# Attention and gated low-rank layer on one core: key operands prepared a chunk ahead, and several side tasks placed at other points

## The chip, the cores and the metric

The kernel runs on one core of one Trainium2 chip. The metric is the device time of one execution in microseconds, as the median of several executions. A profile was taken of one execution; its times start at the first instruction.

## The reference

The input x is (2, 2048, 2048) in float32, that is 4096 tokens of width 2048. All weights are float32.

```python
xn = layernorm(x)                                   # no gain, no bias
# attention, one head of width 512, over 2048 keys of the same batch
q, k, v = split(xn @ Wqkv + bqkv)                   # each (2, 2048, 512)
a = softmax(q @ k^T / sqrt(512)) @ v
attn = a @ Wo + bo
# feed-forward: 64 experts of rank 8, 16 chosen for each token
s = (xn @ Wq^T) @ keys^T                            # (.., 64)
gate = softmax over the 16 greatest of s, 0 elsewhere
z = (xn @ A^T) * repeat(gate, 8)                    # (.., 512)
ffn = (z @ B^T) * 2
out = x + attn + ffn
```

## The kernel before

**Numbers.** Every matrix product is made of float32 operands split into a high part (ScalarE's cast, `split_hi`, line 121 of the profile) and a low part (VectorE's subtraction, `split_lo`, line 124), and of three passes on TensorE (hi by lo, lo by hi, hi by hi). So each operand costs one ScalarE and one VectorE instruction before TensorE can use it.

**Blocks and fast products.** The tokens are 8 blocks of 512. Blocks 0 and 1 go through plain products. The other six go in three pairs (`PAIRS`), each by a scheme that needs seven block products in place of eight (`PHASES`, in the order P1, P2, P6, P5, P3, P7, P4). A phase is six tiles of q, k and z and one of values (`"V"`); beside the products, `beside(j, ph)` gives a list of steps for VectorE and ScalarE, dealt out after each of the phase's seven items.

**Scores.** After the projections, the scores of a pair of query blocks against a pair of key blocks use the same scheme. Their operands are prepared ahead and stored in DRAM. `key_steps(kb, d)` makes those of one chunk, half d of key block kb: two loads (`kr<-k_d`), then for each of seven steps a cast and a subtraction into a tile `kst`, four VectorE sums between them, and seven stores (`kp_d<-kst`), each issued at the next step. There are 16 chunks. `query_steps(j, ring)` makes the query sums of pair j (four loads, four sums, four stores for each half d, tile `qs`). `query_load` and `query_split` bring the operands of one query step into `qt`, and `key_load` brings `kt`.

**The main loop.** The loop over g runs one score product each time (six matmuls of 512 columns, line 1062), 56 for each query pair (NG1 = 56), four pairs. From g = 65 on, `weigh` runs the products of the softmax weights with the values of the pair before (line 129, `acc<-ph,vt`) between them, two or three for one score; value tiles `vt` are loaded three ahead (`load_v`), the weights `ph` are made two ahead (`soft`). The dictionary `side` holds steps to be run after score g; `deal(g, steps, every)` puts them there. `maxes(blk)` finds each query's greatest score on VectorE, and `spread(blk)` is a TensorE product that spreads it over the partitions (tile `mq`, line 1115); `soft` needs the result. After the last score only `weigh` is left (the last values), and beside it `moving` loads and splits the weights of the output stage (`wo`, `wb`) and `ahead` its inputs (`xz`, `s`). `combos` makes sums of output weights for it.

**Queues and order.** Each engine runs its instructions in the order of the program, and nearly all loads and stores are issued by SyncE (SP) in one queue. The order is made by a recording layer from the order of the calls and its own estimates. `behind("sp")`, `behind("pe")` keep what is recorded inside from going ahead of the last instruction so named.

**Slots.** The SBUF memory is a fixed set of named slots (B, 1024 words; G; h and H, about 512). A `Ring` hands them out in turn; a tile that takes a slot waits until the last user of the tile before is done, so a slot that a store still reads holds up its next writer. The ring of the loaded keys is `ks["R"]` (two slots), that of `kst` is `ks["st"]`, that of the values leaving the last phases is `r_vs`. TensorE writes to seven PSUM banks (`acc`).

Of the kernel before, what the change touches and what calls it, by code (L numbers as in the profile page):

```python
# [62 lines left out]
def attn_ffn_kernel(ctx: ExitStack, tc, x, xT, wq, wv, wob, bqk, bv, bo, keysT, out):  # L63
# [17 lines left out]
    def big(*js):  # L81
        return Ring(sb, *(f"B{j}" for j in js))
# [577 lines left out]
    def beside(j, ph):  # L660

        b00, b01, b10, b11 = (0, 0), (0, 1), (1, 0), (1, 1)
        more = j + 1 in PAIRS
        s0, s1 = stat_steps.get(2 * j + 2), stat_steps.get(2 * j + 3)
        if ph == "P1":
            t3 = sum_steps(j, nc.vector, b01, b11, b01, ALU.subtract)
            n10, n01, n11 = x_steps(j, *b10), x_steps(j, *b01), x_steps(j, *b11)
            if j > PAIRS[0]:
                return [], mixed(split_steps(j, "P2", *b10), n01[1], n11[1], t3)
            return (  # L670
                [n10[0], n01[0], n11[0]],
                mixed(n10[1], split_steps(j, "P2", *b10)) + mixed(n01[1], n11[1]),
            )
        if ph == "P2":
            t3 = sum_steps(j, nc.vector, b01, b11, b01, ALU.subtract) if j == PAIRS[0] else []
            return [], mixed(
                t3, sum_steps(j, nc.vector, b00, b01, b00, ALU.add), split_steps(j, "P6", *b00)
            )
        if ph == "P6":
            return [], mixed(  # L680
                sum_steps(j, nc.vector, b10, b10, b00, ALU.subtract),
                sum_steps(j, nc.vector, b00, b11, b00, ALU.subtract), split_steps(j, "P5", *b00),
                s0[:-2] if more else key_steps(0, 0) + key_steps(0, 1) + key_steps(1, 0),
            )
        if ph == "P5":
            if more:
                steps = mixed(split_steps(j, "P3", *b11), s1[:-2])
                return [], s0[-2:-1] + steps[:6] + s0[-1:] + steps[6:]
            return [], mixed(
                split_steps(j, "P3", *b11),  # L690
                [st for m in range(3, 8) for st in key_steps(m // 2, m % 2)],
            )
        if ph == "P3":
            if more:
                n = x_steps(j + 1, *b00)
                steps = mixed(split_steps(j, "P7", *b01), n[1][:2])
                return n[0], s1[-2:-1] + steps[:3] + s1[-1:] + steps[3:]
            return [], mixed(split_steps(j, "P7", *b01), query_steps(0, big(*GROUPS[3])))
        if ph == "P7":
            if more:  # L700
                n = x_steps(j + 1, *b10)
                return n[0], mixed(split_steps(j, "P4", *b10), n[1][:2])
            return [], mixed(split_steps(j, "P4", *b10), query_steps(1, big(*GROUPS[2])))
        if more:
            return x_steps(j + 1, *b01)[0] + x_steps(j + 1, *b11)[0], mixed(
                x_steps(j + 1, *b00)[1][2:], split_steps(j + 1, "P1", *b00)[:2],
            ) + mixed(split_steps(j + 1, "P1", *b00)[2:], x_steps(j + 1, *b10)[1][2:])
        ks["st"] = big(18, 19)
        return [], [lambda: query_load(0, 0)] + mixed(
            [lambda n=n: query_ready(0, n) for n in range(7)], key_steps(4, 0) + key_steps(4, 1)  # L710
        )

    XU, YU, XV, YV = {}, {}, {}, {}
# [106 lines left out]
    ORDER = ("P1", "P6", "P2", "P5", "P3", "P7", "P4")  # L820
    NPAIR = NB // 2
    NKS = NK // 2
    ks = {"R": big(25, 26), "st": big(27, 28, 29, 9)}
    qop, kop = {}, {}

    def key_steps(kb, d):


        v = {}

        def load():
            for h in range(2):
                v[h] = ks["R"]([P, T], F32, "kr")
                nc.sync.dma_start(v[h], k_d[kb][h][:, d, :])
# [27 lines left out]
        return [load] + [lambda step=step: one(step) for step in steps] + [out]  # L862

    def query_steps(j, ring):
# [23 lines left out]
        return steps(0) + steps(1)  # L888

    def query_load(j, n):  # L890

# [97 lines left out]
    for j in PAIRS:  # L989
        for ph in PHASES:  # L990
            if j == PAIRS[-1] and ph == "P4":
                sA, sB, sC, sD = GROUPS
                r_qt = big(*sC, *sD, *sA, *sB)
                r_kt = big(*T_SLOTS[:3], 25, 26)
            n = phase(j, ph, n)


# [11 lines left out]
    r_tp = mid(0, 1, 2, 3)  # L1009
    r_ph = wide(0, 1, 2)  # L1010
    r_vt = wide(3, 4, 5, 9)
    ks = {"R": mid(0, 1), "st": wide(0, 1, 2, 3, 4, 5)}
    S, tag_of, mbc, pt_, M, L, av, rl_, vt_, lsum = {}, {}, {}, {}, {}, {}, {}, {}, {}, {}
    ones = mid(2)([P, P], F32, "ones")
    nc.vector.memset(ones, 1.0)
# [384 lines left out]
        for k, st in enumerate(steps):  # L1400
            side.setdefault(g + k * every, []).append(st)

    for n, (kb, d) in enumerate(((5, 0), (5, 1), (6, 0), (6, 1))):
        deal(2 + 11 * n, key_steps(kb, d))

    def small_ring():
        ks["st"] = mid(2, 3)

    deal(NG1 + 10, [small_ring] + key_steps(7, 0) + key_steps(7, 1))
    deal(NG1 + 38, query_steps(2, r_tp), 2)  # L1410
    deal(2 * NG1 + 7, query_steps(3, r_tp), 2)
    slots = [NG1 + 51, *(2 * NG1 + k for k in (20, 37, 43, 49)), *(3 * NG1 + k for k in (7, 13, 19))]
    for k, g in enumerate(slots):
        deal(g, combos(k // ND, k % ND), 2)

    for j in range(1, NPAIR):
        deal(NG1 * j - 14, [lambda j=j: query_load(j, 0), lambda j=j: query_split(j, 0)], 4)
        for n in range(1, 7):
            deal(NG1 * j - 7 + n, [lambda j=j, n=n: query_load(j, n), lambda j=j, n=n: query_split(j, n)], 3)
    deal(begin[0] - 8, [lambda c=c: load_v(c) for c in range(3)])  # L1420
    deal(begin[0] - 3, [lambda c=c: soft(c) for c in range(2)])
    done = 0
    for g in range(begin[-1]):
# [6 lines left out]
            with behind("sp"):  # L1430
                st()
        if j and j <= NPAIR:
            if n == 1:
                maxes(2 * j - 2)
            if n in (0, 2):
                with behind("pe"):
                    spread(2 * j - 1 - n // 2)
        if n == NG1 - 2 and j < NPAIR:
            maxes(2 * j + 1)
        for i in range(NPAIR - 1):  # L1440
# [20 lines left out]
    slots = [*qt_, *b_[2:], *ph_, *vt2_[:3]]  # L1461
    r_tm = [slots_of(*slots[4 * n : 4 * n + 4]) for n in range(len(STEPS))]
    r_xo = half(0, 1, 2, 3, 4, 5, 6, 7)
    while done < NW * NPAIR:
        weigh(done)
        done += 1
        c, d = divmod(done - NW * (NPAIR - 1), ND)
        if d == 0 and c in (2, 6, 10, 14):
            for kk in range(0, ND, 2):
                with behind("sp"):  # L1470
                    for st in moving(0, STEPS[c // 4], kk):
                        st()
        if d == 0 and c == 18:
            load_bo(0)
        if d == 0 and c in (20, 24, 28):
            ahead(c // 4 - 5)
# [75 lines left out]
```

## Time and profile before

| | |
|---|---|
| median of 3 runs | 2652.06 us (2650.37 to 2656.02) |
| profiled execution | 2654.26 us, span 2652.4 us from first to last instruction |
| mean granted TensorE clock | 0.991 |
| TensorE busy with matmuls | 2604.3 us, 98% |
| VectorE, ScalarE, GpSimd busy | 1982.9, 858.9 and 519.9 us |
| projections, last pair from phase P6 on | 1110 to 1333 us of the span |
| scores alone (g = 0 to 64) | 1333 to 1450 us |
| scores and weighting by turns | 1450 to 1924 us |
| last values | 1924 to 2039 us |
| output stage | 2039 us to the end |

How to read the rows that follow later. A row of the timeline has its start in us, its length, the engine, the line of the kernel, the operation, output<-inputs, and the number of instructions merged; in square brackets is how long the engine sat idle before it and what ended that. A row of the waits has who waited, for whom, the total in us, how often, and the longest. A row of a table by stretches has the busy time (and number of instructions) of TensorE, its weight loads, VectorE, ScalarE and GpSimd, then the granted clock, the share of the DMA engines and GB/s.

### The profile page before, as it was taken

The numbers are of one execution on the slowest core, as the hardware profiler recorded it, in microseconds if no ns is written. First come the engines' busy times: TensorE is split into PE (matmuls) and PEld (weight loads), VectorE is DVE, ScalarE is ACT, GpSimd is POOL, SyncE is SP. The second block draws the span as 40 slices with busy tenths as digits, with TensorE's granted clock in tenths as the row PEclk, the third lists the DMA queues.
The fourth block names the chain that finished last, engine by engine and source line by source line (L and its number), as shares of the span: only waits on it lengthen the run. The fifth ranks groups of instructions, "written<-read, shape, count | busy, mean of one in ns | idle before, by whom it ended". The sixth has DMA issues, their size and how long they took to land. (4 is left out here: it accounts for less than half of the span.)

```text
span 2652.4 us, 34800 instructions
## 1 busy us (share of the span) xinstructions
PE 2604.3 (98%) x12689; PEld 2197.6 (83%) x12689; DVE 1982.9 (75%) x2827; ACT 858.9 (32%) x1249; POOL 519.9 (20%) x315
## 2 busy tenths in 40 slices
PE   8999999999999999999989999999999999999999
PEld 7889888888888889888867887878877888888887
DVE  6557539867868678776778979979698766797675
ACT  4223223323332323343323423334254222232221
POOL 1311420001000010000000000000000756566654
PEclk9999999999999999999999999999999999999999
DMA  6667874667446673688999898888578545565542
GB/s 233 228 246 260 286 273 170 221 217 266 146 155 221 219 256 121 195 260 284 313 284 313 251 316 294 272 311 297 178 270 291 177 166 171 175 218 175 179 160 102
DMA packets 348043, 608.10 MB, mean 229 GB/s; under 512 B 28456, under 2 KB 151392, under 8 KB 347872
## 3 DMA queue, kind: packets, MB, share of 16 engines
q1 hardware_dynamic: 334912, 575.99, 65.0%
q10 hardware_dynamic: 12960, 29.89, 3.4%
q8 instruction: 100, 1.64, 0.3%
q14 instruction: 71, 0.58, 0.1%
HBM read 450.42 MB, written 155.35 MB: 228 GB/s over the span
## 5 line engine op out<-in xcount | busy, mean ns | idle before, releaser
L129 PE MATMUL acc<-t,pw 128*128 128x512 f32 x3024 | 696.1, 391 | 5.4 <-ACT t L121 4.6
L129 PEld LDWEIGHTS acc<-t,pw 128*128 128x128 f32 x3024 | 566.9, 188 | 124.1 <-ACT t L121 5.0
L1336 PE MATMUL acc<-wb,s 128*128 128x512 f32 x2688 | 609.4, 389 | 0.0
L1336 PEld LDWEIGHTS acc<-wb,s 128*128 128x128 f32 x2688 | 504.7, 188 | 104.6
L1320 POOL TENSOR_TENSOR xo<-xo,bo_bc 128x512 f32<-128x512 f32 x128 | 210.8, 1654 | 914.5 <-DMA bo_bc<-in_bo 609.6
L129 PE MATMUL acc<-ph,vt 128*128 128x512 f32 x1536 | 381.0, 393 | 6.1 <-DMA vt<-v_d 2.8
L1062 PE MATMUL acc<-qt,kt 128*128 128x512 f32 x1344 | 342.1, 397 | 16.9 <-ACT sp L1069 10.3
L129 PEld LDWEIGHTS acc<-ph,vt 128*128 128x128 f32 x1536 | 290.3, 190 | 69.7 <-ACT ph L121 3.1
L1062 PEld LDWEIGHTS acc<-qt,kt 128*128 128x128 f32 x1344 | 256.1, 192 | 77.0 <-ACT sp L1069 11.8
L121 ACT CAST pw<-pw 128x1024 fp32r<-128x1024 f32 (+1 forms) x168 | 177.7, 1058 | 343.7 <-PE acc L129 231.9
L124 DVE TENSOR_TENSOR pw<-pw 128x1024 fp32r<-128x1024 f32 (+1 forms) x168 | 214.2, 1276 | 71.9 <-ACT pw L121 68.8
L129 PE MATMUL acc<-xh,wh 128*128 128x512 f32 x1152 | 263.6, 390 | 0.0
L129 PEld LDWEIGHTS acc<-xh,wh 128*128 128x128 f32 x1152 | 215.6, 188 | 44.9
L129 PEld LDWEIGHTS acc<-pw,t 128*128 128x128 f32 x2016 | 247.3, 189 | 3.9 <-DVE yv L755 2.6
L129 PE MATMUL acc<-pw,t 128*128 128x264 f32 x2016 | 248.3, 285 | 2.3 <-DVE yv L755 2.3
L121 ACT CAST s<-xz 128x1024 fp32r<-128x1024 f32 x112 | 118.0, 1054 | 373.4 <-PE acc L1336 313.2
L124 DVE TENSOR_TENSOR s<-xz,s 128x1024 fp32r<-128x1024 f32 x112 | 170.1, 1520 | 43.5 <-ACT s L121 43.5
L124 DVE TENSOR_TENSOR wh<-wu,wh 128x512 fp32r<-128x512 f32 x96 | 81.0, 860 | 99.4 <-ACT wh L121 99.4
L518 POOL TENSOR_TENSOR zt<-zt,g 128x512 f32<-128x512 f32 x24 | 39.0, 1633 | 517.2 <-DMA g<-gd 285.1
L121 ACT CAST ph<-sp 128x512 fp32r<-128x512 f32 x128 | 78.9, 619 | 167.2 <-PE acc L129 161.1
L1325 DVE TENSOR_TENSOR xo<-xo,acc 128x512 f32<-128x512 f32 x128 | 86.9, 680 | 54.8 <-PE acc L1336 26.0
L121 ACT CAST t<-xq 128x1024 fp32r<-128x1024 f32 x84 | 88.0, 1051 | 94.3 <-DVE xq L648 41.0
(165 smaller groups left out, 2525.3 us busy)
## 6 DMA issues: line engine op xcount, KB each, us to landing
vt<-v_d SPq DMA_DIRECT2D x128, 512.0 KB, 4.7
kt<-kp_d SPq DMA_DIRECT2D x224, 256.0 KB, 5.4
pw<-sq_d SPq DMA_DIRECT2D x72, 512.0 KB, 4.1
xo<-in_x SPq DMA_DIRECT2D x128, 256.0 KB, 3.2
xz<-oz_d SPq DMA_DIRECT2D x64, 512.0 KB, 4.5
out_y<-xo SPq DMA_DIRECT2D x128, 256.0 KB, 2.5
kp_d<-kst SPq DMA_DIRECT2D x112, 256.0 KB, 3.7
pw<-in_wq SPq DMA_DIRECT2D x54, 512.0 KB, 4.3
```

The costliest lines, as they stand in the source:

```text
L121: return nc.scalar.copy(hi, src)
L124: return (eng or nc.vector).tensor_tensor(lo, src, raw(hi), ALU.subtract)
L129: last["pe"] = nc.tensor.matmul(ps, st(a_), mv(b_), start=first and n == 0, stop=end and n == 2)
L518: nc.gpsimd.tensor_tensor(zt, zt, gx[n], ALU.mult)
L1062: last["pe"] = nc.tensor.matmul(ps, k[:, a, d, :], q[c][:, d, :], start=not more and d == 0 and i == 0, stop=d == 1 and i == 2, skip_group ...
L1320: nc.gpsimd.tensor_tensor(xs, xs, bo_bc[q // (NB // 2 * NH), c], ALU.add)
L1325: nc.vector.tensor_tensor(xs, xs, ps, op)
L1336: nc.tensor.matmul(ps, st[a_][:, kk, sl], mv[b_], start=not more and kk == 0 and n == 0, stop=kk == ND - 1 and n == 2, skip_group_check=more,)
```

## The change

- `key_steps` gives its load apart from its steps. The ring of loaded keys gets four slots (B25, B26, H7, H8 in the projections; the four h slots in the first 56 scores; two again from g = NG1 + 2). `key_list` puts the load of the next chunk after the third step of the chunk before. In the main loop a chunk's load stands three scores ahead of its first step (six for chunks 9 to 11).
- The chunks are spread differently: phases P6, P5, P3, P7, P4 of the last pair had 3, 5, 0, 0 and 2 of them and now have 3, 2, 0, 2 and 1 (`kst` gets three slots in P4 instead of two). The main loop takes 8 instead of 6: four in the first 56 scores as before, then chunks 12, 13 and 14 in the next 56, and 15 at the start of the third 56.
- The query sums of pair 0 are split over P3 and P7 (they were all in P3), those of pair 1 move from P7 to P4 and its end, in the four h slots.
- In P4 the values leave through `r_ev`, four slots, instead of two.
- `maxes` of the even block comes one score later (n = 2, not 1); `spread` comes at n = 1 and 4, not 0 and 2.
- The splits of pair 1's query operands come five scores after their loads, not three (the first five, not four).
- `combos` and the later `query_steps` run their three steps at distances 3 and 1 instead of 2 and 2, at other scores: five of the eight `combos` now fall after g = 168, where three did.
- The eight output loads of `moving` before the output stage come singly, at c = 1, 3, .. 15 of the last values, and their splits three values later, at c = 4, 6, .. 18; before, two loads with their splits came together at c = 2, 6, 10 and 14.

```diff
 def beside(j, ph):   # the last pair's branches
-                s0[:-2] if more else key_steps(0, 0) + key_steps(0, 1) + key_steps(1, 0),    # P6
+                s0[:-2] if more else key_list(0, 3),
-                [st for m in range(3, 8) for st in key_steps(m // 2, m % 2)],                # P5
+                key_list(3, 5)
-            return [], mixed(split_steps(j, "P7", *b01), query_steps(0, big(*GROUPS[3])))    # P3
+                split_steps(j, "P7", *b01), query_steps(0, big(*GROUPS[3]), (0,))
-            return [], mixed(split_steps(j, "P4", *b10), query_steps(1, big(*GROUPS[2])))    # P7
+                split_steps(j, "P4", *b10), query_steps(0, big(*GROUPS[3]), (1,)), key_list(5, 7)
-        ks["st"] = big(18, 19)                                                               # P4
+        ks["st"] = Ring(sb, "H6", "B18", "B19")
-            [lambda n=n: query_ready(0, n) for n in range(7)], key_steps(4, 0) + key_steps(4, 1)
+            [lambda n=n: query_ready(0, n) for n in range(7)],
+            key_list(7, 8, False) + query_steps(1, mid(0, 1, 2, 3)),
...
-    ks = {"R": big(25, 26), "st": big(27, 28, 29, 9)}
+    ks = {"R": Ring(sb, "B25", "B26", "H7", "H8"), "st": big(27, 28, 29, 9)}
+    def key_list(a, b, more=True):
+        for k in range(a, b + 1):
+            if k not in KEYS:
+                KEYS[k] = key_steps(k // 2, k % 2)
+        steps = [KEYS[a][0]] if a == 0 else []
+        for k in range(a, b):
+            ops = list(KEYS[k][1])
+            if k + 1 < b or more:
+                ops.insert(3, KEYS[k + 1][0])
+            steps += ops
+        return steps
...
+                r_vs = r_ev                       # from P4 of the last pair on
...
-    ks = {"R": mid(0, 1), "st": wide(0, 1, 2, 3, 4, 5)}      # main loop
+    ks = {"R": mid(0, 1, 2, 3), "st": wide(0, 1, 2, 3, 4, 5)}
...
-    for n, (kb, d) in enumerate(((5, 0), (5, 1), (6, 0), (6, 1))):
-        deal(2 + 11 * n, key_steps(kb, d))
+    def keys(k, g, load):
+        first, steps = key_steps(k // 2, k % 2)
+        deal(load, [first])
+        deal(g, steps)
+    def spaced(g, steps):
+        for k, st in enumerate(steps):
+            deal(g + (0, 3, 4)[k % 3] + 5 * (k // 3), [st])
+    for n in range(4):
+        keys(8 + n, 3 + 11 * n, 11 * n - 3 if n else 0)
-    deal(NG1 + 10, [small_ring] + key_steps(7, 0) + key_steps(7, 1))
-    deal(NG1 + 38, query_steps(2, r_tp), 2)
-    deal(2 * NG1 + 7, query_steps(3, r_tp), 2)
-    slots = [NG1 + 51, *(2 * NG1 + k for k in (20, 37, 43, 49)), *(3 * NG1 + k for k in (7, 13, 19))]
+    deal(NG1 + 2, [small_ring])
+    for n, g in ((12, NG1 + 6), (13, NG1 + 18), (14, NG1 + 49), (15, 2 * NG1 + 10)):
+        keys(n, g, g - 3)
+    spaced(NG1 + 36, query_steps(2, r_tp))
+    spaced(2 * NG1 + 19, query_steps(3, r_tp))
+    slots = [2 * NG1 + k for k in (35, 40, 45)] + [3 * NG1 + k for k in (7, 12, 17, 22, 35)]
     for k, g in enumerate(slots):
-        deal(g, combos(k // ND, k % ND), 2)
+        spaced(g, combos(k // ND, k % ND))
-        deal(NG1 * j - 14, [load of operand 0, split of operand 0], 4)     # lambdas, shortened
+        deal(NG1 * j - 14, [load of operand 0, split of operand 0], 5)
         for n in range(1, 7):
-            deal(NG1 * j - 7 + n, [load of operand n, split of operand n], 3)
+            deal(NG1 * j - 7 + n, [load of operand n, split of operand n], 5 if j == 1 else 3)
...
-            if n == 1:
+            if n == 2:
                 maxes(2 * j - 2)
-            if n in (0, 2):
+            if n in (1, 4):
                 with behind("pe"):
-                    spread(2 * j - 1 - n // 2)
+                    spread(2 * j - 1 - n // 4)
...
-        if d == 0 and c in (2, 6, 10, 14):
-            for kk in range(0, ND, 2):
-                with behind("sp"):
-                    for st in moving(0, STEPS[c // 4], kk):
-                        st()
+        if d == 0 and 1 <= c <= 18:
+            k, part = (c - 1) // 2, (c - 1) % 2
+            if part == 0:
+                if k < 8:
+                    half_of[k] = moving(0, STEPS[k // 2], 2 * (k % 2))
+                    with behind("sp"):
+                        half_of[k][0]()
+            elif k:
+                half_of[k - 1][1]()
```

More of the change, by code (lines that the diff above doesn't have):

```diff
@@ L688, in beside @@
                 return [], s0[-2:-1] + steps[:6] + s0[-1:] + steps[6:]
-            return [], mixed(
-                split_steps(j, "P3", *b11),
-                [st for m in range(3, 8) for st in key_steps(m // 2, m % 2)],
-            )
+            return [], mixed(split_steps(j, "P3", *b11), key_list(3, 5))
         if ph == "P3":
@@ L697, in beside @@
                 return n[0], s1[-2:-1] + steps[:3] + s1[-1:] + steps[3:]
-            return [], mixed(split_steps(j, "P7", *b01), query_steps(0, big(*GROUPS[3])))
+            return [], mixed(
+                split_steps(j, "P7", *b01), query_steps(0, big(*GROUPS[3]), (0,))
+            )
         if ph == "P7":
@@ L702, in beside @@
                 return n[0], mixed(split_steps(j, "P4", *b10), n[1][:2])
-            return [], mixed(split_steps(j, "P4", *b10), query_steps(1, big(*GROUPS[2])))
+            return [], mixed(
+                split_steps(j, "P4", *b10), query_steps(0, big(*GROUPS[3]), (1,)), key_list(5, 7)
+            )
         if more:
@@ L861, in key_steps, with query_steps @@
         steps = ("P1", "P2", "P4", "P5", "P7", "P6", "P3")
-        return [load] + [lambda step=step: one(step) for step in steps] + [out]
-    def query_steps(j, ring):
+        return load, [lambda step=step: one(step) for step in steps] + [out]
+    KEYS = {}
+    def key_list(a, b, more=True):
[9 more added lines that the diff above has]
+        return steps
+    def query_steps(j, ring, ds=(0, 1)):
         def steps(d):
@@ L886, in steps @@
             return [load, sums, out]
-        return steps(0) + steps(1)
+        return [st for d in ds for st in steps(d)]
     def query_load(j, n):
@@ L1401, in deal @@
             side.setdefault(g + k * every, []).append(st)
-    for n, (kb, d) in enumerate(((5, 0), (5, 1), (6, 0), (6, 1))):
-        deal(2 + 11 * n, key_steps(kb, d))
-    def small_ring():
-        ks["st"] = mid(2, 3)
-    deal(NG1 + 10, [small_ring] + key_steps(7, 0) + key_steps(7, 1))
-    deal(NG1 + 38, query_steps(2, r_tp), 2)
-    deal(2 * NG1 + 7, query_steps(3, r_tp), 2)
-    slots = [NG1 + 51, *(2 * NG1 + k for k in (20, 37, 43, 49)), *(3 * NG1 + k for k in (7, 13, 19))]
+    def keys(k, g, load):
[7 more added lines that the diff above has]
+        keys(8 + n, 3 + 11 * n, 11 * n - 3 if n else 0)
+    def small_ring():
+        ks["R"], ks["st"] = mid(0, 1), mid(2, 3)
+    deal(NG1 + 2, [small_ring])
[4 more added lines that the diff above has]
+    slots = [2 * NG1 + k for k in (35, 40, 45)] + [3 * NG1 + k for k in (7, 12, 17, 22, 35)]
     for k, g in enumerate(slots):
-        deal(g, combos(k // ND, k % ND), 2)
+        spaced(g, combos(k // ND, k % ND))
     for j in range(1, NPAIR):
-        deal(NG1 * j - 14, [lambda j=j: query_load(j, 0), lambda j=j: query_split(j, 0)], 4)
+        deal(NG1 * j - 14, [lambda j=j: query_load(j, 0), lambda j=j: query_split(j, 0)], 5)
         for n in range(1, 7):
-            deal(NG1 * j - 7 + n, [lambda j=j, n=n: query_load(j, n), lambda j=j, n=n: query_split(j, n)], 3)
+            deal(
+                NG1 * j - 7 + n, [lambda j=j, n=n: query_load(j, n), lambda j=j, n=n: query_split(j, n)],
+                5 if j == 1 else 3,
+            )
     deal(begin[0] - 8, [lambda c=c: load_v(c) for c in range(3)])
@@ L1463, in attn_ffn_kernel @@
     r_xo = half(0, 1, 2, 3, 4, 5, 6, 7)
+    half_of = {}
     while done < NW * NPAIR:
```

## The prediction

> **What bounds the kernel now.** First the page's busy rows: TensorE is busy 98%, and only it. Then TensorE's own waits, since only they can be won back:
>
> ```profile
> PE 2604.3 (98%) x12689; PEld 2197.6 (83%) x12689; DVE 1982.9 (75%) x2827; ACT 858.9 (32%) x1249; POOL 519.9 (20%) x315
> ...
> PE acc L1062 <- ACT sp L1069: 10.3, 3, 5.9
> PE misc L1115 <- DVE mq L1105: 4.7, 4, 1.8
> PE acc L129 <- ACT t L121: 4.6, 1, 4.6
> PE acc L1062 <- DVE qt L124: 4.4, 5, 1.3
> PE acc L129 <- DMA vt<-v_d: 2.8, 1, 2.8
> PE acc L129 <- DVE yv L755: 2.3, 1, 2.3
> ```
>
> Almost all of these lie between 1110 and 2039 us, where the change works. The timeline of the longest shows the mechanism:
>
> ```profile
> 1338.22 11.70 PE L1062 MATMUL acc<-qt,kt 128*128 128x512 f32 x42 [2.47 <-ACT sp L1069]
> ...
> 1346.42 0.43 DVE L288 TENSOR_TENSOR vs<-acc,xv 128x264 f32<-128x264 f32 x1 [7.53 <-DMA v_d<-vs]
> ...
> 1351.46 1.12 SPq L834 DMA_DIRECT2D kr<-k_d  x2
> ...
> 1354.90 0.40 ACT L121 CAST kst<-kr 128x256 fp32r<-128x256 f32 x1 [6.75 <-DMA kr<-k_d]
> 1355.21 0.58 ACT L1069 COPY sp<-acc 128x512 f32<-128x512 f32 x1
> ```
>
> VectorE waits 7.53 us because the third `vs` tile needs a slot that a store still reads (two slots). The key load is issued at 1351.46, when those same slots are free, and ScalarE waits 6.75 us for it at a `kst` cast. Behind the cast stands the copy of a score (L1069), which P2 of the next group must have: TensorE idles 5.92 us. Then the tables by stretches, for the cover:
>
> ```profile
> 1336.00:1346.00 10.00, 7.78 (x27) 6.34 (x28) 2.57 (x6) 1.33 (x4) 0.00 (x0) 0.83 0.97 299
> 1333.00:1390.00 57.00, 46.68 (x187) 36.33 (x186) 37.41 (x76) 13.27 (x32) 0.00 (x0) 0.91 0.90 284
> 1390.00:1450.00 60.00, 53.59 (x213) 41.12 (x212) 50.94 (x93) 19.78 (x33) 0.00 (x0) 0.95 0.94 323
> 1780.00:1850.00 70.00, 70.00 (x308) 57.72 (x309) 67.95 (x99) 26.93 (x37) 0.00 (x0) 1.00 0.88 300
> ```
>
> The granted clock falls after a gap; and VectorE, 37.4 + 50.9 = 88.3 us busy in the 117 us of scores alone, is nearly as loaded as TensorE: undisturbed, six matmuls start every 1.36 us, and 65 scores need 65 x 1.36 = 88.4 us.
>
> **What the skill says.** The Trainium skill, "TensorE: Matmul & The Clock Gate", Part 1, says that the clock halves after idling and that the windows are about 3.4 us. The trace agrees: a mean of 0.83 over 10 us is 1.7 us lost, 3.4 us at half. So I price a gap of about 2 us or more at itself **plus 1.7 us**. "PSUM — Partial Sum Buffer", Engine vs sequencer instructions, says that ScalarE and VectorE work in strict order; the L1069 row, free only after the `kst` cast, agrees. "DMA: Bandwidth & Descriptors", Issuing engines are not separate DMA queues, says that all transfers share the same 16 engines; before the 2.76 us gap at 1956 two `wo` loads of 512 KB stand among the `vt` loads, and the DMA engines are full (1.00 busy, 391 GB/s from 1956 to 1964), which fits.
>
> **The account of lost time**, from TensorE's timeline. The excess is the length of the run after a gap less (matmuls x 0.2267 us + 0.16), the pace of undisturbed runs.
> - P6 and P5: gaps 4.59 + 2.25, excess 2.3 + 0.8 = 9.9 us.
> - Scores alone: gaps 2.47 + 5.92 + 1.92 (ScalarE late), 1.85 (`kt`), 4.35 in five pieces (`qt` splits), excess 2.0 + 2.05 + 1.7 + 1.7 = 24.0 us.
> - By turns: `mq` 1.82 with 1.8 excess, 1.77 and 0.32, 0.26 after the first; 1.38 at 1530 behind a 3.35 us reciprocal. 7.35 us.
> - Last values: `mq` 0.76; `vt` 2.76 + 1.7; `ph` 1.92 + 1.8. 8.9 us.
>
> Together 50 us, the most that the change can win.
>
> **The change part by part.**
> *Key loads ahead, four slots, fewer chunks in P5.* No work is removed: 16 chunks of 7 casts and 11 VectorE operations of 0.42 us stay. The 51.3 us of ScalarE's wait for `kr` (21 times) should go, as a load (5.1 us to land) gets about five steps of a chunk, or three to six scores, of lead. In P5 the chunks fall from five to two, 3 x 4.6 = 13.8 us less on VectorE; P7, where VectorE was busy 29.8 of 45 us, takes 2 x 4.6 - 2.7 (query sums net) = 6.5 us more: covered. Won: 8 of 9.9.
>
> *Four value slots and early key loads at the start of the scores.* The third `vs` no longer waits, the key loads no longer need the `vs` slots, and in the changed program's order no `kst` cast stands between the value casts and the first score copy. Of 2.47 + 5.92 + 2.0 + 2.05 = 12.4 I take 10. The 1.92 + 1.7 was the same wait at the third chunk (7.38 us for `kr`): 3.5. The `kt` gap, 1.85 + 1.7, began with SP held from 1402 to 1406 by a `kst` store waiting for a late key: 2.5.
>
> *Query splits two scores later.* The load gets 1.36 x 2 = 2.7 us more, which ends ScalarE's waits (22.1 us for `q_d`). But the split now stands two scores before its use instead of four, on a VectorE that is full there (7 x 1.22 us of splits beside `maxes`). Bound: +3 to -4 us; I take 0. Sum for scores alone: 16.
>
> *Spreads one or two scores later.* One score is 1.36 us alone and about 3 us with its weighting, more than each `mq` wait. `soft` needs the result only some 9 us before its own use. Of 1.82 + 1.8 + 0.26 + 1.77 + 0.32 + 0.76 = 6.7 I take 6; 1530 stays.
>
> *Output loads one at a time.* One `wo` (1.3 us at 391 GB/s) instead of two stands ahead of the `vt` loads at the change of block, and in the changed order one more `vt` goes before the store that held SP from 1949 to 1952. Behind the reciprocal (3.35 us) the next `ph` subtraction comes first instead of two `wb` of 1.22 us. Of 8.2 I take 6.
>
> *What it costs.* (a) The second half of pair 1's query sums now stands between the value steps and the first score sum on VectorE, and its loads stand on SP behind the stores that free their slots, with `kt` behind them: store 2.0 to 6.6 us, load as much; banks and the order of steps cover about 6. Between 0 and 7: 3. (b) Chunk 12 starts beside the last query splits, chunk 14 beside the next pair's: 4.6 us each on VectorE. Between 0 and 5: 2. (c) Two more `combos` after g = 168, 8 x 0.69 = 5.5 us, largely where VectorE is busy 67.95 of 70 us; the seven banks absorb most. Between 0 and 5: 2. Together 7 (0 to 17).
>
> Sum: 8 + 16 + 6 + 6 - 7 = **29 us won**. The profiled execution took 2654.26 us (span 2652.4), 2.2 above the median; it would become 2625, the median **2623**.
>
> **The rivals.**
> *VectorE takes over.* With the waits gone, VectorE (88 us) and TensorE (88 us) compete in the scores alone; the `qt` burst and chunk 12 stretch it. For: the five `qt` gaps. Against: it idled 4 us and more at `kr` and `vs`. Then that stage gives 6 instead of 16, and (b), (c) cost 3 more: 29 - 13 = 16, a median of 2636. Chance 0.20.
>
> *Slower: SP held by early loads.* An early load whose slot is not free yet holds SP's queue, and `vt`, `kt` and `pw` behind it. A `vt` has 3 x 2.72 - 4.7 = 3.4 us to spare; a hold past that, by 0.6 us, costs 0.6 + 1.7 = 2.3 us of TensorE. To cancel 29 us and lose 6 more, all 15 early loads must do so (15 x 2.3 = 35): 2658. Against: with four slots the slot was left a whole chunk ago; with two (chunks 12 to 15) only a VectorE lagging two scores and 3.4 us, 9 us, would do it. Chance 0.08.
>
> *The stalls only move*, as ScalarE and VectorE were late for other reasons: within 5 us of 2652. Chance 0.05.
>
> **How the numbers follow.** The forecast has 0.67; its own range is 29 - 10 to 29 + 14, so 2609 to 2633 (the latter part if nearly all 50 are won and (a) to (c) cost 7). Down to one in ten left out on each side, the range takes in the first rival: **2608 to 2644**. A difference of 0.2%, 5.3 us, is about what a measurement of this kernel can tell. Faster by more: 0.67 + 0.20 = 0.87; the same: 0.05; slower: 0.08.
>
> **What would show it.** ScalarE's wait for `kr` below 15 us (51.3); VectorE's `vs` wait for `v_d` below 8 (19.0); no gap over 3 us between 1333 and 1350; `mq` waits below 1 us (4.7); TensorE's clock in the scores alone above 0.97 (0.91, 0.95); no long `vt` wait after 1924. Wrong, if `qs` or `qt` appear as new releasers of over 8 us in the scores, or SP's waits ahead of `kr` loads grow and `vt` waits with them.

## The result and the profile after

The changed kernel takes 2642.99 us (median of 6 runs, 2638.84 to 2645.26), the kernel before 2655.52 us in the runs beside it (6 runs, 2650.37 to 2660.36). The ratio is 0.9952, 95% interval 0.9937 to 0.9967: about 12.5 us faster, where 29 were forecast. The profiled execution took 2639.59 us (span 2637.8), 14.6 us less in span than before, so the two profiles show a difference of the right size.

The page's busy row and TensorE's own waits (who, for whom, us in total, times, longest):

```profile
PE 2600.1 (99%) x12689; PEld 2194.4 (83%) x12689; DVE 1994.4 (76%) x2827; ACT 860.0 (33%) x1249; POOL 523.7 (20%) x315
...
PE acc L1081 <- DMA kt<-kp_d: 5.5, 2, 4.7
...
PE acc L129 <- ACT pw L121: 3.7, 1, 3.7
PE misc L1134 <- DVE mq L1124: 2.7, 3, 1.1
...
PE acc L1081 <- DVE qt L124: 2.2, 4, 0.7
```

The score copies (10.3 us before), `yv` and most of `vt` are gone. In their place stand two long waits: 4.7 us for a key tile `kt` (the longest such wait was 1.9 us before), and 3.7 us for the cast of value weights `pw`, which the kernel before did not have. The rows for ScalarE and VectorE that I had named as marks, with one on store slots between them:

```profile
ACT kst L121 <- DMA kp_d<-kst: 29.7, 18, 4.3
ACT kst L121 <- DMA kr<-k_d: 19.3, 12, 4.2
...
DVE vs L288 <- DMA v_d<-vs: 8.8, 11, 2.4
```

ScalarE's wait for key loads fell from 51.3 to 19.3 us (I had said below 15), its wait for the slot of a `kst` store rose from 23.9 to 29.7; VectorE's wait for a `vs` slot fell from 19.0 to 8.8 (I had said below 8). Two more marks failed clearly: a gap of 4.66 us stands between 1333 and 1350 (none over 3), and the `mq` waits are 2.7 us (below 1). The long `vt` wait after 1924 is gone, as I had said. The table by stretches, columns as before:

```profile
1336.00:1346.00 10.00, 7.71 (x34) 6.02 (x33) 5.87 (x12) 1.62 (x4) 0.00 (x0) 1.00 0.95 324
1333.00:1390.00 57.00, 51.51 (x228) 41.84 (x228) 44.51 (x89) 15.52 (x36) 0.00 (x0) 0.97 1.01 337
1390.00:1450.00 60.00, 56.43 (x233) 44.02 (x232) 55.06 (x97) 22.04 (x36) 0.00 (x0) 0.97 0.91 321
```

TensorE gained 4.8 us of work in the first stretch of scores alone and 2.8 in the second, and its clock rose from 0.91 and 0.95 to 0.97. VectorE is now busy 55.06 of 60 us in the second.

**The account by stretch.** For each pair of neighbouring matmuls I take the time from start to start less the undisturbed pace (0.227 us for 512 columns, 0.1225 for 264) and add it up. It includes the half clock after a gap, and the edges of the stretches are fixed times, so a microsecond can fall on either side. Each column is one profile; "again" is a second profile of the changed kernel (run i0 below), and e1, f1, h1 and h2 are experiments below.

| lost TensorE time, us | before | changed | again | e1 | f1 | h1 | h2 |
|---|---|---|---|---|---|---|---|
| P6, P5 (1110 to 1200) | 9.7 | 6.1 | 4.8 | 4.0 | 2.4 | 1.5 | 0.4 |
| P3, P7 (1200 to 1299) | 1.1 | 0.3 | 0.3 | 6.7 | 6.3 | 7.1 | 6.4 |
| P4 with its values (1299 to 1333) | -0.2 | 7.2 | 8.8 | -0.2 | -0.1 | -0.2 | -0.1 |
| scores alone (1333 to 1450) | 27.1 | 15.3 | 16.0 | 11.0 | 8.3 | 10.3 | 8.6 |
| by turns (1450 to 1915) | 10.1 | 11.1 | 7.2 | 13.2 | 8.1 | 12.6 | 12.9 |
| last values (1915 to 2045) | 10.5 | 4.4 | 4.7 | 5.4 | 6.1 | 7.0 | 3.5 |
| sum | 58.3 | 44.4 | 41.8 | 40.1 | 31.1 | 38.3 | 31.7 |

58.3 - 44.4 = 13.9 us, against 14.6 in the spans. One line is new and large: P4 had no loss and now has 7 to 9 us. With it the projections lose more than before: from 1110 to 1333 it was 10.6 us, now 13.6 and 13.9, so that all of the gain comes from the scores and the last values. The timeline in P4 (start, length, engine, operation, in brackets the idle time before it and what ended that):

```profile
1316.21 2.14 SPq L892 DMA_DIRECT2D qs<-q_d  x4
...
1317.08 5.97 PE L129 MATMUL acc<-pw,t 128*128 128x264 f32 x48
...
1318.40 0.43 SPq L915 DMA_DIRECT2D qt<-qs_d  x1
...
1318.87 0.43 SPq L605 DMA_DIRECT2D pw<-in_wv  x1
...
1324.28 1.04 ACT L121 CAST qt<-qt 128x1024 fp32r<-128x1024 f32 x1 [9.04 <-DMA qt<-qs_d]
1325.61 1.07 ACT L121 CAST pw<-pw 128x1056 fp32r<-128x1056 f32 x1 [0.29 <-DMA pw<-in_wv]
...
1326.74 0.39 PE L129 MATMUL acc<-pw,t 128*128 128x264 f32 x1 [3.69 <-ACT pw L121]
```

Read it upwards. TensorE waits 3.69 us for the second half of the value weights to be cast. ScalarE does that cast at 1325.61, right behind the cast of a query operand for which it sat idle 9.04 us. That operand was issued at 1318.40, behind four query tiles (1 MB) of pair 1's sums, which the change moved here from P7. The same place in the kernel before:

```profile
1318.47 0.43 SPq L605 DMA_DIRECT2D pw<-in_wv  x1
...
1321.25 11.77 PE L129 MATMUL acc<-pw,t 128*128 128x264 f32 x96
...
1324.34 1.08 ACT L121 CAST pw<-pw 128x1056 fp32r<-128x1056 f32 x1 [0.94 <-DMA pw<-in_wv]
```

The load of the second half is issued at nearly the same time, and from its issue to its cast 5.9 us pass there and 6.7 us here. What differs more is TensorE: it begins the products of the first half at 1321.25 in the kernel before, 2.8 us after that issue, and at 1317.08 in the changed one, 1.8 us ahead of it. Nor were the DMA engines fuller (1290 to 1333 us; first row before, second row after):

```profile
1290.00:1333.00 43.00, 43.00 (x236) 37.63 (x235) 30.73 (x52) 19.31 (x30) 2.65 (x2) 1.00 0.97 314
1290.00:1333.00 43.00, 38.06 (x195) 32.72 (x194) 28.54 (x45) 16.08 (x21) 2.53 (x2) 0.96 0.91 301
```

So the time that TensorE had won up to here is lost again, because the weights are issued too late for it. Then the first scores:

```profile
1333.92 2.39 SPq L892 DMA_DIRECT2D qs<-q_d  x4
...
1339.24 2.32 SPq L902 DMA_DIRECT2D qs_d<-qs  x2
...
1344.36 1.30 SPq L937 DMA_DIRECT2D kt<-kp_d  x2
...
1348.38 2.18 PE L1081 MATMUL acc<-qt,kt 128*128 128x512 f32 x5 [4.66 <-DMA kt<-kp_d]
```

The second half's loads and stores, and the value stores among them, hold SP from 1333.92 to 1344.3, with only one key tile let through; the next two are issued at 1344.36, and TensorE has its tile 4 us later.

### The profile page after: what moved, and what is told of

It reads as the page before. It is cut to its first block, busy times and chain, and to the rows that moved or that the text cites. A ratio compares the mean times of both kernels' runs of the same rounds, so it can differ in the third digit from the quotient of the medians.

```text
span 2637.8 us, 34791 instructions
## 1 busy us (share of the span) xinstructions
PE 2600.1 (99%) x12689; PEld 2194.4 (83%) x12689; DVE 1994.4 (76%) x2827; ACT 860.0 (33%) x1249; POOL 523.7 (20%) x315
## 5 line engine op out<-in xcount | busy, mean ns | idle before, releaser
L518 POOL TENSOR_TENSOR zt<-zt,g 128x512 f32<-128x512 f32 x24 | 40.1, 1683 | 507.1 <-DMA g<-gd 241.4
L124 DVE TENSOR_TENSOR t<-xq,t 128x1024 fp32r<-128x1024 f32 x84 | 107.5, 1283 | 18.6 <-ACT t L121 18.1
```

The source lines that it names most:

```text
L124: return (eng or nc.vector).tensor_tensor(lo, src, raw(hi), ALU.subtract)
L518: nc.gpsimd.tensor_tensor(zt, zt, gx[n], ALU.mult)
```

## The experiments

Ratios are to the kernel before, with 95% intervals; the changed kernel has 0.9952 (0.9937 to 0.9967). 0.001 is 2.65 us. Unless said otherwise an edit is to the changed kernel.

**i0: the changed kernel again.** No edit.

> The changed kernel once more, unaltered. If its first profile's stalls in P6 (6 us lost from 1110 to 1200) and at the third pair's block change (6 us from 1835 to 1870) belong to it, they come again; if they are chance, 1 to 3 us each are lost, as in the kernels that share the code there. The ratio should be 0.995 (0.9937 to 0.9967 before); 0.993 would mean that the forecast was missed by 5 us less.

0.9952 (0.9937 to 0.9967). The loss at the third pair's block change was 2.1 us this time, so 4 us of the first profile's 6.0 were chance. That from 1110 to 1200 came again, 4.8 (6.1), though eight other runs below with the same code there show 1.0 to 4.0; why stays open. The losses in P4 and at the first scores came again, larger.

**e1: pair 1's query sums back in P7, pair 0's wholly in P3.**

```diff
-query_steps(0, big(*GROUPS[3]), (0,))                      # P3
+query_steps(0, big(*GROUPS[3]))
-query_steps(0, big(*GROUPS[3]), (1,)), key_list(5, 7)      # P7
+query_steps(1, big(*GROUPS[2])), key_list(5, 7)
-key_list(7, 8, False) + query_steps(1, mid(0, 1, 2, 3))    # P4
+key_list(7, 8, False)
```

> Pair 1's query sums are formed in P7 again, pair 0's wholly in P3, as in the kernel before; the rest stays as changed. Theory: the four query loads ahead of the value weights in P4 and the two stores ahead of the key tiles at the first scores are what TensorE waits for there. The 4.66 us gap on kt at 1348 and the 3.69 us gap on the pw cast at 1327 both go, the wait of ScalarE's qt cast for its load (9.04 us) falls below 4, and the kernel gains 8 to 11 us on the changed one: a ratio of about 0.991 to the kernel before. Rival: the values start 4 us earlier than in the kernel before, so the weights and key tiles are late in any case, or the sums in P7 delay the operands there; then the gaps stay or move and the ratio stays within 0.001 of 0.995.

0.9932 (0.9914 to 0.9949). Both stalls went, P4 lost nothing and the scores 11.0 us instead of 15.3. But a gap of 4.18 us on the `pw` cast appeared at 1281 in P7, where the four query loads again stood between the two halves of the value weights. From 1200 to 1333 the loss is 6.5 us, against 7.5 in the changed kernel: the stall at the key tiles is gone, that at the weights has moved with the sums. And the rival had a part in it: TensorE, held up in P7, begins the last values of P4 at 1321.98, as late as in the kernel before, and the cast of their second half comes no earlier than in the changed kernel (1325.29 and 1325.61). The edit also gives the sums their old slots back, so place and slots are not told apart.

**f1: the same, with the loads placed early in P7.**

```diff
+ks2 = key_list(5, 7)
-query_steps(1, big(*GROUPS[2])), key_list(5, 7)
+mixed(query_steps(1, big(*GROUPS[2])), ks2[:6]) + ks2[6:]
```

> Pair 1's query sums are formed in P7 again, but its loads, sums and stores are set beside the first six key steps, so that the last load of four query tiles (1 MB) is issued before the values' weights and not between their two halves. Theory: what TensorE waited for in P4, at the first scores, and in P7 in the run where the sums stood there evenly, was each time one megabyte of query loads and the key load next to it ahead of the second half of the value weights (or the key tiles) on SP. Then no gap of over 1 us is left on the pw cast or on kt from 1260 to 1350, some 11 us less lost than in the changed kernel, ratio 0.990 to 0.992. Rival: ScalarE's cast list in P7, with two key chunks, is what is late; then a gap of 3 to 5 us stays in P7 as with the even placing, ratio 0.993.

0.9938 (0.9925 to 0.9951). From 1299 to 1450 only 8.2 us are lost (22.5 in the changed kernel), but P7 still loses 6.3, in pieces of about 1 us. Its timeline:

```profile
1256.13 2.06 SPq L894 DMA_DIRECT2D qs<-q_d  x4
...
1262.52 0.69 DVE L897 TENSOR_TENSOR qs<-qs 128x512 f32<-128x512 f32 x1 [4.05 <-DMA qs<-q_d]
...
1263.26 0.41 ACT L121 CAST kst<-kr 128x256 fp32r<-128x256 f32 x1 [8.84 <-DVE qs L897]
...
1268.52 5.78 PE L129 MATMUL acc<-t,pw 128*128 128x512 f32 x24 [0.86 <-DVE pw L124]
```

Setting the steps closer together had put the sums only 6.4 us behind their loads. VectorE stood still for 4.05 us, ScalarE's key cast for 8.84, and the weights' casts behind it came late. So P7 still loses time, as the rival had it, but for a reason of my own making.

**h1: loads a full item ahead of their sums, and eight store slots in P6 and P5.**

```diff
+q, k = query_steps(1, big(*GROUPS[2], *GROUPS[3])), key_list(5, 7)
-query_steps(1, big(*GROUPS[2])), key_list(5, 7)            # P7 as in e1
+[q[0], *k[:3], q[3], *k[3:6], q[1], k[6], q[2], k[7], q[4], k[8], q[5], *k[9:]]
-"st": big(27, 28, 29, 9)                                   # this ring again from P7 on
+"st": Ring(sb, "B27", "B28", "B29", "B9", "H6", "H0", "H1", "H2")
```

> Best version so far of the earlier place: pair 1's query sums in P7, with both query loads set in the phase's first two items (into the slots of two groups, so that the second needs none of the first's stores) and each at least one item of 10 us ahead of its sums; and eight store slots for the keys in P6 and P5. Theory: in the run with early loads the sums stood only 6 us after their loads, VectorE waited 4.05 us for them, and the keys' casts and the casts of the weights behind it (8.84 us on ScalarE) made the 6.3 us lost in P7; with the lead that goes to 1 to 2 us and the gain over the changed kernel is 8 to 11 us: ratio 0.991 to 0.992. Rival: P7 with two key chunks and the query sums has too much work for VectorE and ScalarE; then 5 us or more stay lost from 1200 to 1299 and the ratio is 0.9935 to 0.994.

0.9908 (0.9890 to 0.9926), median 2629.70: some 24 us faster than before, 12 faster than the changed kernel, with intervals that do not overlap. By the ratio the theory's range holds. Its profiled execution, at 2636.55 the slowest of its six, does not show P7 clear: 7 us are lost from 1200 to 1299. Of these, 2.6 us are for a weight piece whose load stood on SP behind the item's query and key loads. On this point the rival holds: h2 below, with the same P7, loses 6.4.

**i1: only the order of the loads within P4.** The first half's loads after four key steps instead of eight, the sums after seven.

```diff
-key_list(7, 8, False) + query_steps(1, mid(0, 1, 2, 3))
+k[:4] + q[:1] + k[4:7] + q[1:2] + k[7:] + q[2:]            # k, q: the two lists above
```

> The query sums of pair 1 stay in P4, but the first half's four loads are issued after four of the phase's key steps instead of after eight, ahead of both halves of the value weights by more than an item, and its sums after seven; the second half stays where it was. Theory: the order of the loads alone makes the stall, as 1 MB of query tiles and an operand of 512 KB stand ahead of the second half of the weights; then the wait on the pw cast (3.7 us) and the 7.2 us lost from 1299 to 1333 go, the gap on kt at the first scores (4.7 us) stays, and 5 to 7 us are won: ratio 0.993. Rival: ScalarE's list in P4 (seven query splits) is late by itself; then 5 us or more stay lost there, ratio 0.995.

0.9952 (0.9938 to 0.9966): nothing won. The stall moved one piece of weights ahead:

```profile
1301.01 0.46 SPq L917 DMA_DIRECT2D qt<-qs_d  x1
...
1307.37 1.04 ACT L121 CAST qt<-qt 128x1024 fp32r<-128x1024 f32 x1 [6.75 <-DMA qt<-qs_d]
...
1311.04 1.22 PE L129 MATMUL acc<-t,pw 128*128 128x512 f32 x2 [3.91 <-DVE pw L124]
```

The ratio is the rival's: my theory of this one order fell. The last piece of weights is now issued 2.9 us ahead of its item and makes no stall, but the piece before it stands on SP behind the query loads instead. P4 is the phase in which seven query operands of 512 KB are loaded, each cast by ScalarE ahead of a piece of weights. In both orders the `qt` behind the extra 1 MB is late, and the `pw` cast stands behind it.

**k1: in the kernel before, the four value slots alone.**

```diff
 r_kt = big(*T_SLOTS[:3], 25, 26)
+r_vs = r_ev
```

> The kernel before with one line of the change: the values of P4 get the four slots of the feature results, so the first key load of the scores no longer shares slots with them. My forecast gave four value slots and early key loads together 10 of 12.4 us at the first scores. If the shared slots made that stall, the two gaps of 2.47 and 5.92 us between 1333 and 1356 shrink to under 3 in sum and 6 to 10 us are won on the kernel before: ratio 0.9965 to 0.9975. If the key load's own lateness makes it, the 5.92 us gap stays and the ratio is 0.999 to 1.0.

0.9982 (0.9973 to 0.9991): 4.8 us, between the two. The gaps were 3.11 and 4.33 us, for 2.47 and 5.92:

```profile
1353.39 0.41 ACT L121 CAST kst<-kr 128x256 fp32r<-128x256 f32 x1 [6.78 <-DMA kr<-k_d]
...
1361.47 2.93 PE L1063 MATMUL acc<-qt,kt 128*128 128x512 f32 x6 [4.33 <-ACT sp L1070]
```

With the slots free the key load is issued at 1346 instead of 1351, and is still 6.78 us late for its cast. This profile is the slowest of its 22 runs, 7 us above their median, and the two gaps sum to 7.4 us, against 8.4. So the slots alone do not remove that stall; that the load's place beside its own first step makes the rest is argued from the timeline, as no run has the early loads without the slots.

**g1: two slots for loaded keys again**, the new dealing kept.

```diff
-Ring(sb, "B25", "B26", "H7", "H8")   and   mid(0, 1, 2, 3)
+big(25, 26)                          and   mid(0, 1)
```

> The key loads have two slots again (one chunk), so that a chunk's load cannot start before the chunk ahead of it is done, with the new dealing of the chunks kept. My forecast gave the early loads with four slots most of 8 us in P6 and P5 and part of 10 + 3.5 us at the scores. If the slots are what counts, ScalarE's wait for kr comes back above 40 us (19.3 in the changed kernel) and 8 to 12 us are lost: ratio 0.999. If the even dealing alone did it, under 3 us are lost, ratio 0.9955.

0.9964 (0.9954 to 0.9974), 3 us slower than the changed kernel with intervals that overlap. ScalarE waits 24.2 us for `kr`, not 40 or more. So the four slots took away little of the 51.3 us. The rest went with the new dealing, in which the loads also stand earlier in the order; and with the value slots, since k1 alone has 37.4.

**e3: eight store slots for the keys in P6 and P5** (the last lines of h1's diff alone).

> The ring of split key tiles that are stored has eight slots instead of four while chunks 0 to 4 are formed (P6 and P5). Theory: the store slots are the wait that took the place of the load's wait; the 4.26 us wait of ScalarE for a kst slot at 1141 and the gaps of TensorE at 1150 and 1151 (1.81 + 1.26 and half the clock) go, 4 to 5 us gained (ratio about 0.9935). Rival: ScalarE and VectorE are late there by the order of their steps (two difference steps on VectorE ahead of each operand split), and the gaps stay within 1 us; ratio 0.995.

0.9944 (0.9928 to 0.9961), not to be told from 0.9952. The loss from 1110 to 1299 was 1.0 us, but e4, e5 and e6 below, with four slots, show 1.3 to 1.5. What the slots are worth stays open.

**e5: the spreads back at scores 0 and 2, the maxes at 1.**

```diff
-if n == 2: maxes(2 * j - 2)
+if n == 1: maxes(2 * j - 2)
-if n in (1, 4): spread(2 * j - 1 - n // 4)
+if n in (0, 2): spread(2 * j - 1 - n // 2)
```

> The spreads stand at scores 0 and 2 and the maxes at 1 again, as in the kernel before, the rest as changed. My forecast gave moving them 6 of 6.7 us: then the kernel is 4 to 6 us slower than the changed one, ratio 0.997. The runs since then show mq waits of 2.7 to 4.5 us in the changed kernel too, so the rival is that one score of lead is eaten by VectorE's backlog and the move is worth 1 to 2 us: ratio 0.9955.

0.9948 (0.9936 to 0.9961): no loss. The `mq` waits rose to 4.6 us, from 2.7 in both profiles of the changed kernel, so the move had shortened the waits by 2 us; yet the time lost by turns is 9.7 us, between those two (11.1 and 7.2).

**f2: the spreads later still**, at scores 3 and 8, maxes at 5, the weighting of the middle pairs two scores later.

```diff
-if n == 2: maxes(2 * j - 2)
+if n == 5: maxes(2 * j - 2)
-if n in (1, 4): spread(2 * j - 1 - n // 4)
+if n in (3, 8): spread(2 * j - 1 - n // 8)
```

> The spreads stand at scores 3 and 8 after the change of pair (1 and 4 in the changed kernel), the first block's maxes at score 5 (2), and the weighting of the two middle pairs begins two scores later. Theory: the mq chain is late because VectorE has a backlog of query splits and sums ahead of it; each score beside weighting gives it about 3 us, so the three mq waits (4 us with 1 to 2 us more lost each) go, 4 to 6 us gained, ratio 0.993 to 0.994. Rival: with the spread later the softmax steps behind it come later too and TensorE waits for ph or sp instead, ratio 0.995 or more.

0.9962 (0.9950 to 0.9974), nothing won. TensorE's waits from 1450 to 1915:

```profile
PE acc L129 <- DVE sp L1105: 2.8, 3, 1.2
PE acc L129 <- DVE sp L1091: 2.3, 1, 2.3
...
PE misc L1134 <- DVE mq L1124: 0.9, 1, 0.9
```

The `mq` waits there halved (1.9 us in the changed kernel), and waits for VectorE's score sums (`sp`, first row) came up near them: of the three, two stand at 1604 and 1773, shortly after the changes of pair. The second row stands at 1862, at the third pair's block change, where the changed kernel stalls too. It fits that VectorE is behind and TensorE waits for it under one name or another; as the start of the weighting moved as well, the run does not show it alone.

**e6: the output loads back, two at a time.** The block after `half_of` is again that of the kernel before.

> The output weights are loaded and split two at a time at steps 2, 6, 10 and 14 of the last values, as in the kernel before, the rest as changed. My forecast gave this part 6 of 8.2 us. If it holds, 4 to 6 us are lost again after 1915, with waits for vt (2.8 us) and ph (1.9 us): ratio 0.997. Rival: the last values' waits came from the key chunks and combinations ahead of them, and nothing is lost: ratio 0.995.

0.9964 (0.9954 to 0.9974), 3 us slower than the changed kernel with intervals that overlap. The last values lose 11.5 us instead of 4.4 and 4.7, and the two stalls of before return:

```profile
1941.51 0.43 SPq L1264 DMA_DIRECT2D wo<-in_wob  x1
1942.03 3.69 SPq L1177 DMA_DIRECT2D vt<-v_d  x4
...
1947.97 28.39 PE L129 MATMUL acc<-ph,vt 128*128 128x512 f32 x117 [2.60 <-DMA vt<-v_d]
...
1985.43 6.93 PE L129 MATMUL acc<-ph,vt 128*128 128x512 f32 x22 [2.46 <-DVE ph L124]
```

**e4: pair 1's splits close to their loads again** (`5` to `3` and `4`).

> Pair 1's query splits stand three scores (four for the first) after their loads again, as in the kernel before, the rest as changed. My estimate of this part was 0, with bounds of +3 and -4 us. If the longer lead helps, ScalarE's waits for qt loads near 1420 come back and the kernel is 2 to 4 us slower than the changed one (ratio about 0.9965). If the later place beside VectorE's full list is what makes the qt gaps at 1420 (1.4 + 0.66 + 0.67 and half the clock), they shrink and it is 2 to 4 us faster (0.994). If neither, 0.995.

0.9955 (0.9939 to 0.9972): no difference. The second stretch of scores alone lost 6.7 us, against 7.6 and 7.1.

**e2: one combination moved off the third pair's block change**, from 3 NG1 + 35 to 3 NG1 + 44.

> One of the eight output-weight combinations is moved from the score at which the third pair changes its block (3 NG1 + 35) to nine scores later (3 NG1 + 44). Theory: VectorE has no room at that block change, and the four sums put there (2.8 us) delay the reciprocal and so the first bank of the new block; the stall of 1.84 + 0.80 us with half the clock near 1855 goes, a gain of 4 to 6 us (ratio about 0.993). Rival: the reciprocal of 3.35 us alone makes that stall, or all the sums of this stretch do; then the stall stays within 1 us of what it was, ratio 0.995.

0.9953 (0.9938 to 0.9967). 2.9 us were lost there, against 6.0 and 2.1 without the edit: nothing shown.

**h2: h1 with four combinations before the last change of pair and three before the block change.**

```diff
-slots = [2 * NG1 + k for k in (35, 40, 45)] + [3 * NG1 + k for k in (7, 12, 17, 22, 35)]
+slots = [2 * NG1 + k for k in (30, 35, 40, 45)] + [3 * NG1 + k for k in (7, 13, 19, 44)]
```

> The best version so far (query sums in P7 with lead, eight store slots), and four of the eight output-weight combinations before the last change of pair and three after it ahead of the block change (slots 2 NG1 + 30, 35, 40, 45 and 3 NG1 + 7, 13, 19, 44; the changed kernel has three and five). My forecast charged the five with 2 us (0 to 5). If VectorE's backlog there makes the stall at the third pair's block change (2 to 6 us in the runs), that stall falls below 1 us and 2 to 4 us are won: ratio 0.9895. If the earlier combination only loads VectorE where the mq chain of the pair's change waits for it, the stall moves there: ratio 0.991.

0.9915 (0.9900 to 0.9931), the same as h1. The stall at the block change is gone (3.9 us in h1, 0.04 here), but at 1727 TensorE now waits 2.59 us for a `vt` that SP could issue only behind the four loads of a combination (3.29 us). It moved.

## Why the prediction was wrong, step by step

The sign was right, and three of the five parts. The step that failed most is what the prediction charged for work moved into P7 and P4: nothing. It called P7 "covered" by VectorE's free time, and priced pair 1's query sums only for their second half. P4 then lost 8 us; a gain of 6 us was not there, and one of 8 us came out at half.

- **Work moved into P7 and P4 (0 charged): failed.** These two phases, with P3, lost 0.9 us before and lose 7.5 and 9.1 now. The first half of the sums went into P4 with its 1 MB of loads, and I did not go through what SP issues and ScalarE casts behind it. The timelines show how it costs time: from issue to cast the last piece of weights takes 6.7 and 7.3 us, and 6.6 to 7.3 us in e1, f1, h1 and h2, where the sums are elsewhere. But it is issued 1.8 and 2.0 us after TensorE has begun the item's first half, and in those four 3.3 to 4.5 us before. So the load is no slower than in those runs, it is issued too late. That the place of the sums decides where this happens is shown by e1, f1, h1 and i1. That the sums alone make it is not: in every version of the changed kernel 6.1 to 9.5 us are lost between 1200 and 1333, in P7 or in P4, and all of them have three key chunks in these two phases, two of them in P7, where the kernel before had two, both in P4. No run took a chunk out, so which of the moved work has no room there stays open.
- **Key loads and fewer chunks in P5 (8 of 9.9): half of it.** The loss from 1110 to 1200 fell from 9.7 to 6.1 and 4.8 us: 3.6 and 4.9 won. Eight other runs with the same code there lost 1.0 to 4.0, so 8 can be reached; what makes the difference is not known. The reason given was half right: by g1 the four slots did little.
- **Scores alone (16 won, 3 lost again as cost (a)): net nearly right, both terms too small.** The stretch went from 27.1 to 15.3 and 16.0, so 11 to 12 won net, against 13. With the sums elsewhere it loses 8.3 to 11.0, so the other parts were worth 16 to 19 and cost (a) 5 to 7, at the upper end of its bound of 7, and by the mechanism that I gave: from 1333 to 1350, around the `kt` stall, the changed kernel lost 5.7 and 5.9 us, those four runs 0 to 1.1. That the value slots and the early loads were each needed is not shown (k1 and g1 each tell of one part only).
- **Spreads later (6 of 6.7): failed.** The `mq` waits fell by 2 us, not by 4, and undoing the move (e5) costs nothing measurable. I read `mq` as a chain that needed one more score of lead. The table had VectorE busy 67.95 of 70 us right after one of these waits (1780 to 1850), and I had used that number only for the combinations; that VectorE's next result is late instead fits f2.
- **Output loads one at a time (6 of 8.2): right**, 6.8 to 7.1 us in that stretch by e6, though the ratios of whole runs give 3.
- **Query splits (0): right**, by e4.
- **Costs (b) and (c) (4 together): not resolved.** The losses by turns are 11.1 and 7.2 us in two profiles of one kernel, against 10.1 before, so the profile cannot hold such terms apart. Only the third pair's block change stands out: the kernel before lost nothing there, the changed one 6.0 and 2.1, and h2, with fewer combinations ahead of it, nothing. But e5, with the changed kernel's combinations, lost only 0.3.

By stretch, with the mean of the two profiles: P6 and P5 won 4 where 8 were forecast, P3 to P4 lost 7 where nothing was, the scores alone won 11.5 for 13, the part by turns 1 for 2 (6 for the spreads less 4 of costs), the last values 6 for 6. That makes 15 for 29; whole runs give 12.5 (8.8 to 16.7). That the part by turns comes out so close is luck, as the gain is not shown and neither are all of its costs.

Of the rivals, "VectorE takes over" gave 2636, 7 us from the result, but not by its mechanism: it let the scores alone win 6, and they won 11 to 12 even with the query sums beside them. What it said of the `qt` burst does hold, as 6.7 to 7.9 us were lost from 1390 to 1450 in every variant of the changed kernel, some of them waits for `qt` on VectorE and ScalarE. "SP held by early loads" meant the key loads; SP was held, ahead of `kt` and `pw`, but by the loads and stores of the query sums. And "the stalls only move" is what e1, i1, f2 and h2 show of single stalls, and what happened to the gain of P6 and P5, though not to the whole.

## What to carry to other kernels

When a step is moved, price all of it at the place where it arrives: each load it puts into the queue, what stands behind that load on the issuing queue, and which in-order engine has the late tile ahead of something urgent. Free time of the compute engines does not answer this: here a piece of weights was issued 1.8 us after TensorE had begun its item, took 6.7 us to its cast, and stopped TensorE for 3.69 us. Time won ahead of such a place is not yet won, since TensorE only arrives there earlier. And before a wait on an engine's result is given more lead, look at how busy that engine is: here, where VectorE had been busy 97% of a stretch, asking later shortened the waits by 2 us and won nothing.

## What the runs showed of the hardware

In these runs the price of the clock after a gap did not follow from the gap. (Gaps are here from start to start, less the pace.) In e2 the gaps of 1.6 and 1.5 us at 1146 and 1148 were followed by no slow matmul; in the first profile of the changed kernel, gaps of 2.0 and 1.5 us at the same place were followed by 13 matmuls at half the clock, 2.6 us. The same pair of gaps at the first `qt` (1.55 and 0.93 us) was followed by 8 slow matmuls in the first profile and by none in e2 and i0. The Trainium skill, "TensorE: Matmul & The Clock Gate", Part 1, says that the window which the hardware watches runs freely, so that its place relative to the kernel differs from run to run; these runs agree. The gaps named here are all shorter than the 3.4 us that the prediction took from that section, and some were followed by the half clock all the same. The 1.7 us that I added to each gap of 2 us is therefore a mean at best, and differences of 3 us between two single profiles, as at the third pair's block change (6.0 and 2.1 us for one kernel), need a second profile before they are given a cause.
